# Later due times for the layer norms' powers in a planned attention and gated-graph kernel

## The chip, the cores and the metric

The kernel runs on one core of one Trainium2 chip. The metric is the device time of one execution in microseconds, as a median over runs. In the text PE is TensorE, DVE is VectorE, ACT is ScalarE, POOL is GpSimd and SP is SyncE. Of SyncE, only the issuing of DMAs matters here.

## The reference

The input x has shape (16, 1024, 128): 16 samples of 1024 nodes with 128 features. The matrix adj (1024 x 1024) holds zeros and ones. Two layers follow each other, each with a residual and a layer norm over the features:

```
h = x @ others_weight;  u1 = h @ a1;  u2 = h @ a2
e = leaky(u1[idx1] + u2[idx2]);  att = softmax(where(adj > 0, e, -9e15), axis=1)
x = layernorm(x + att @ h + x @ self_weight)            # layer 0

repeat 5 times, from h = x:                             # layer 1
    m = adj @ h             # both messages use the same adj
    z = sigmoid([m, m] @ w3.T + b3 + u);  r = sigmoid([m, m] @ w4.T + b4 + u);  u = h @ u3.T + bu3
    v = tanh([m, m] @ w5.T + b5 + (r * h) @ u5.T + bu5)
    h = (1 - z) * h + z * v
out = layernorm(x + h)
layernorm(x) = (x - mean(x)) / sqrt(var(x) + 1e-5)
```

Everything is float32.

## The kernel before

**Tiles and stages.** The 16 samples are called b. `layer0(b)` does the attention of one sample and its layer norm, which the profile calls "y". Layer 1 goes by pairs q of samples (2q, 2q + 1) and steps s from 0 to 4. `messages(q, s, k)` forms the products with adj for a pair; for most steps it saves multiplications by working with sums of blocks. `gates(b, s, soon)` does the gates r and z and the new state hT for each half e of the nodes. `leave(b, s)` brings the new state back into the other layout for the next step, through DRAM: VectorE transposes blocks of 32 (tile T), SyncE stores them (tile X), and the next step loads them as G. After the last step, `leave` adds the residual, which had been put aside in DRAM as yd, to give the tile o, and calls the layer norm "o". GpSimd then issues the output DMA. The last two samples take another way out (`end`).

**A layer norm** handles half a sample, 4 blocks of 128 nodes, in three operations on three engines. `look` (lines 527 and 529, VectorE) finds the mean and the variance. `power` (lines 533 to 543, GpSimd) makes rstd = (var + eps) to the power -0.5 and the bias. `scale` (line 548, ScalarE) applies them with four activations of 128 x 128. After a "y" scaling come the store of yd by GpSimd (L1009), the store of X by SyncE (L1023), and a block transpose on VectorE (tile T_b), which goes through DRAM (D_b, stored on L589, and F_b, loaded on L597) and becomes hT by a copy on ScalarE (L1037). After an "o" scaling comes only the output DMA (L1344). The tile o has two buffers. SyncE loads yd into it (L1324), and a pair needs four such halves.

**Order of the work.** No engine's order is written out by hand. Each operation is handed to `plan.add` with an engine, an assumed length in ns, a rank, and what it reads and writes. `Plan.order` simulates the engines with those lengths. When an engine is free, it takes the ready operation of the lowest rank for which buffers are free. The order of these starts is the program's order on every engine, and on the chip each engine keeps to it, waiting for semaphores. How long after an operation's assumed end its users count as ready is `LAG[engine]` (200 ns for POOL), unless the operation was given a `lag` of its own:

```
lag = self.SAME[engine] if ops[u][0] == engine else self.LAG[engine]
lag = self.lag.get(i, lag)
```

A `power` has an assumed length of 3001 ns (2301 in the short form, which only the last half of the last sample uses). Operations of VectorE and ScalarE get 10% on top of their assumed length, and TensorE's users of them 400 ns more (`CARE`).

**Names in the profile.** L621 is the helper `product` (all products with adj, and its sums), L1189, L1199, L1215 and L1216 are the gates' matmuls, L571 a transpose on TensorE. L1192 is the copy gz, L1114, L1141 and L1143 the copies of messages m, L1202 and L1221 the activations of the gates, L609 and L613 the two halves of a split for the products, L1083 a sum of G tiles. L1209, L1224, L1227 and L1230 are VectorE's part of the gates, with two inputs in SBUF each. L579 is the block transpose on VectorE.

Of the kernel before, what the change touches and what calls it, by code (L numbers as in the profile page):

```python
# [137 lines left out]
def kernel(  # L138
# [79 lines left out]
    def exact(pools):  # L218
# [67 lines left out]
        plan = Plan({tag: k[0] for tag, k in kinds.items()})  # L286
# [16 lines left out]
        D = dict(m=-0.8, pu=1.4, u=0.8, pr=0.8, pz=1.2, r=1.7, pv=1.0, z=1.3, hv=-0.4, h=1.2, tr=1.6, o=6.6, ln=2.9)  # L303
# [13 lines left out]
        def rank0(b):  # L317
            return 10 * (b // 2) - 1 * (1 - b % 2) + -1.0 - 6 * (b // 2 == 1)

        def sign(b):  # L320

            return 1 if b % 2 else -1
# [17 lines left out]
        def early_loads():  # L340
# [28 lines left out]
            writes=[(boot, "early"), (ws, "early"), (x0, "early"), (("xt", 1), "early"), *((t, "early") for k in staged for t in k)],  # L369
# [149 lines left out]
                dve(V, 1 + c / 4, sum_, reads=[*y, *more], writes=[(("tab",), c, n)])  # L519


        def layernorm(key, g, rank, after, src, dst, write, sg=1, short=False, later=()):
            stats, mv, rstd = ("stats", *key, g), ("mv", *key, g), ("rstd", *key, g)

            def look():
                for j in range(4):
                    nc.vector.bn_stats(T(stats)[:, j, :], src(j))
                for j in range(4):
                    nc.vector.bn_aggr(T(mv)[:, j, :], T(stats)[:, j, :])  # L529

            def power():
                mean, var, r = T(mv)[:, :, 0], T(mv)[:, :, 1], T(rstd)
                nc.gpsimd.tensor_scalar(r[:, 0, :], var, EPS, None, ALU.add)  # L533
                nc.gpsimd.tensor_tensor(r[:, 0, :], r[:, 0, :], mhalf[:, 0:4], ALU.pow)
                if short:
                    if sg < 0:
                        nc.gpsimd.tensor_scalar(r[:, 0, :], r[:, 0, :], -1.0, None, ALU.mult)
                elif sg > 0:
                    nc.gpsimd.tensor_scalar(r[:, 1, :], mean, -1.0, None, ALU.mult)
                    nc.gpsimd.tensor_tensor(r[:, 1, :], r[:, 1, :], r[:, 0, :], ALU.mult)  # L540
                else:
                    nc.gpsimd.tensor_tensor(r[:, 1, :], mean, r[:, 0, :], ALU.mult)
                    nc.gpsimd.tensor_scalar(r[:, 0, :], r[:, 0, :], -1.0, None, ALU.mult)

            def scale():
                r = T(rstd)
                for j in range(4):
                    nc.scalar.activation(
                        dst(j), src(j), AF.Identity, bias=r[:, 1, j : j + 1], scale=r[:, 0, j : j + 1]
                    )  # L550

            def scale_short():
                for j in range(4):
                    nc.vector.tensor_scalar(
                        dst(j), src(j), T(mv)[:, j, 0:1], T(rstd)[:, 0, j : j + 1], ALU.subtract, ALU.mult
                    )

            after = after if isinstance(after, list) else [after]
            dve(1100, rank, look, reads=after, writes=[(stats, 0), (mv, 0)])
            plan.add("POOL", 2301 if short else 3001, rank, power, reads=[(mv, 0)], writes=[(rstd, 0)])  # L560
            if short:
                dve(900, rank, scale_short, reads=[*after, (mv, 0), (rstd, 0)], writes=[write])
            else:
                act(1250, rank, scale, reads=[*after, *later, (mv, 0), (rstd, 0)], writes=[write])
# [66 lines left out]
        def layer0(b):  # L631

            first = rank0(b) - (60 if b == 0 else 0)
            rank = first + D["l1"]
# [9 lines left out]
            yT, y0, yd = ([(k, b, g) for g in range(2)] for k in ("yT", "y0", "yd"))  # L644
# [46 lines left out]
            if b >= 2:  # L691
# [6 lines left out]
                    reads=[(u, 0), (u, 1), (("ident",), 0)],  # L698
                    writes=[(put, 0)],
# [8 lines left out]
                    reads=[(us, 0)],  # L708
                    writes=[(ud, 0)],
# [5 lines left out]
                    reads=[(ud, 0)],  # L715
                    writes=[(pb, 0), (pb, 1)],
                    lag=3000,
# [66 lines left out]
            rank = first + D["l2"]  # L784
# [21 lines left out]
            rank = rank0(b) + D["l2"]  # L806
# [20 lines left out]
            for k in range(2 if b == 0 else 1):  # L827
                cs = slice(4 * k, 4 * k + 4) if b == 0 else slice(0, NC)

                def rz_(k=k, cs=cs):  # L830
# [16 lines left out]
                    reads=[(q, 0), *((zs, c) for c in ks), *((("A",), c, 1) for c in ks)],  # L847
                    writes=[(rz, k), (("bad",), k), (("rstd", "least"), k)] if b == 0 else [(rz, 0), (rz, 1)],
# [3 lines left out]
            rank = rank0(b) + D["l3"]  # L852
# [28 lines left out]
            rank = rank0(b) + D["l4"]  # L881
# [81 lines left out]
            for g in range(2):  # L963
                rank = rank0(b) + D["l5"]

                def y(g=g):
                    return T(yT[g])

                t = ("ps", "t", b, "y", g)
                if on_pe(b, "y"):  # L970
                    transposes(y, [(yT[g], 0)], t, rank)
                else:
                    k, d, t = (x + (b, "y", g) for x in (("T",), ("D",), ("F",)))
                    turn(k, y, [(yT[g], 0)], rank)
                    away(k, d, rank)
                    back(d, t, rank)

                def src(j, t=t, flat=on_pe(b, "y")):
                    return T(t)[:, j * P : (j + 1) * P] if flat else chunks(T(t))[:, j]

                def dst(j, g=g, flat=on_pe(b, "y")):
                    c = T(y0[g])[:, j, :]
                    return c if flat else c.rearrange("p (a j) -> p a j", a=4)

                layernorm(("y", b), g, rank0(b) + D["l6"], (t, 0), src, dst, (y0[g], 0), sign(b))

            if not plain(b // 2, 0):

# [293 lines left out]
        def leave(b, s):  # L1282

            rank = rank_of(b, s)
            hT = ("hT", b)
            for g in range(2):

                def h(g=g):
                    return T(hT)[:, g * HALF : (g + 1) * HALF]

                k, d = ("T", b, s, g), ("X", b, s + 1, g)
                if s < STEPS - 1 and on_pe(b, s):
                    t = ("ps", "t", b, s, g)
                    transposes(h, [(hT, g)], t, rank + D["tr"])
                    split(
                        ("blk", b, "h", s + 1, g),
                        lambda t=t: T(t).rearrange("p (c a j) -> p c a j", c=4, a=4),
                        [(t, 0)],
                        rank_of(b, s + 1),
                    )  # L1300
                    continue
                if s < STEPS - 1:
                    turn(k, h, [(hT, g)], rank + D["tr"])
                    away(k, d, rank + D["tr"])
                    continue

                if b >= B - 2:
                    end(b, s, g, h, rank)
                    continue

                t = ("ps", "t", b, s, g)
                if on_pe(b, s):
                    transposes(h, [(hT, g)], t, rank + D["tr"])
                else:
                    t = ("F", b, s, g)
                    turn(k, h, [(hT, g)], rank + D["tr"])
                    away(k, d, rank + D["tr"])
                    back(d, t, rank + D["o"])

                o, yd = ("o", b, g), ("yd", b, g)  # L1320
                sp(
                    450,
                    rank + D["o"],
                    lambda o=o, yd=yd: nc.sync.dma_start(T(o).rearrange("p c d -> p (c d)"), T(yd)),  # L1324
                    reads=[(yd, 0), (hT, g)],
                    writes=[(o, "y")],
                )

                def last(t=t, o=o, flat=on_pe(b, s)):
                    x = T(o).rearrange("p c (a j) -> p c a j", a=4)  # L1330
                    n = T(t).rearrange("p (c a j) -> p c a j", c=4, a=4) if flat else chunks(T(t))
                    nc.vector.tensor_tensor(x, n, x, ALU.add)

                dve(V, rank + D["o"], last, reads=[(t, 0), (o, "y")], writes=[(o, "raw")])

                def at(j, o=o):
                    return T(o)[:, j, :]

                layernorm(("o", b), g, rank + D["ln"], (o, "raw"), at, at, (o, 0), sign(b))
                plan.add(  # L1340
                    "POOL",
                    900,
                    rank + D["out"],
                    lambda o=o, g=g: nc.gpsimd.dma_start(  # L1344
                        out[b].rearrange("(c p) d -> p c d", p=P)[:, 4 * g : 4 * g + 4, :], T(o)
                    ),
                    reads=[(o, 0)],
                    writes=[((o, "sent"), 0)],
                    lag=2600,
                )  # L1350
# [347 lines left out]
```

## Time and profile before

| what | value |
|---|---|
| median of 3 runs | 1460.33 us (1458.93 to 1460.43) |
| the profiled execution | 1468.01 us, span 1466.2 us |
| TensorE busy | 1440.4 us, 98% of the span |
| VectorE busy | 1160.1 us, 79% |
| ScalarE busy | 896.2 us, 61% |
| GpSimd busy | 203.3 us, 14% |
| granted TensorE clock, mean | 0.994 |
| DMA | 174.20 MB, 119 GB/s |

The span is the time from the first to the last instruction of the profiled execution, which took somewhat longer than the runs without the profiler. A busy share is a mean over all stages. TensorE's busy time contains the modelled ends of its matmuls, so its short gaps are better read from the starts of the matmuls. A line of waits names the waiting engine, its tile and line, who ended the wait, and then the total in us, how often, and the longest.

### The profile page before, as it was taken

The numbers are of one execution on the slowest core, as the hardware profiler recorded it, in microseconds if no ns is written. First come the engines' busy times: TensorE is split into PE (matmuls) and PEld (weight loads), VectorE is DVE, ScalarE is ACT, GpSimd is POOL, SyncE is SP. The second block draws the span as 40 slices with busy tenths as digits, with TensorE's granted clock in tenths as the row PEclk, the third lists the DMA queues.
The fourth block names the chain that finished last, engine by engine and source line by source line (L and its number), as shares of the span: only waits on it lengthen the run. The fifth ranks groups of instructions, "written<-read, shape, count | busy, mean of one in ns | idle before, by whom it ended". The sixth has DMA issues, their size and how long they took to land.

```text
span 1466.2 us, 17789 instructions
## 1 busy us (share of the span) xinstructions
PE 1440.4 (98%) x5020; PEld 902.3 (62%) x5020; DVE 1160.1 (79%) x2753; ACT 896.2 (61%) x1792; POOL 203.3 (14%) x323
## 2 busy tenths in 40 slices
PE   9999999998999999999999999999999999999996
PEld 7766656665566656666666656656566656556663
DVE  5997789868888789987888788896988877776535
ACT  5656465665657665666657576566655656664544
POOL 0311001012101150110201112011200123000201
PEclk9999999999999999999999999999999999999998
DMA  7426135554434643455434543445432554223201
GB/s 250 145 55 205 52 102 150 137 158 116 112 100 137 184 126 90 121 163 150 108 108 123 158 129 101 115 143 159 123 89 79 150 166 129 58 72 87 72 0 31
DMA packets 188032, 174.20 MB, mean 119 GB/s; under 512 B 34239, under 2 KB 137366, under 8 KB 187926
## 3 DMA queue, kind: packets, MB, share of 16 engines
q1 hardware_dynamic: 182562, 156.41, 37.8%
q0 software_dynamic: 4800, 15.73, 3.2%
q8 instruction: 41, 0.67, 0.2%
q10 hardware_dynamic: 564, 0.85, 0.2%
q14 instruction: 65, 0.53, 0.1%
HBM read 95.68 MB, written 77.24 MB: 118 GB/s over the span
## 4 chain that ended last, share of the span: by engine, by line
PE 88%; DVE 4%; DMA 2%; SPq 1%; ACT 1%; issue 1%; POOL 1%; DVEq 0%; POOLq 0%; ACTq 0%
PE ps_acc_a L621 16%; PE ps_g_r L1199 8%; PE ps_g_v L1215 8%; PE ps_g_v L1216 8%; PE gz L1199 8%; PE ps_g_r L1189 8%; PE ps_acc_c L621 8%; PE ps_acc_po L621 8%; PE ps_acc L621 5%; PE gz L621 4%; PE ps_g_ph L658 1%; PE ps_idle L419 1%; SPq L589 1%; PE ps_acc_px L925 1%; PE ps_acc_po L939 1%
## 5 line engine op out<-in xcount | busy, mean ns | idle before, releaser
L1215 PE MATMUL ps_g_v<-m,wm 128*128 128x512 f32 x320 | 163.5, 592 | 0.1
L1216 PE MATMUL ps_g_v<-r,u5h 128*128 128x512 f32 x320 | 163.4, 592 | 0.0
L1199 PE MATMUL ps_g_r<-m,wm 128*128 128x512 f32 x320 | 160.0, 593 | 2.6 <-ACT gz L1192 2.6
L1199 PE MATMUL gz<-m,wm 128*128 128x512 f32 x320 | 159.5, 592 | 0.0
L1189 PE MATMUL ps_g_r<-hT,u 128*128 128x512 f32 x320 | 153.3, 592 | 0.0
L1224 DVE TENSOR_TENSOR hv<-hv,hT 128x512 f32<-128x512 f32 x160 | 109.8, 686 | 51.5 <-ACT hv L1221 51.0
L621 PE MATMUL ps_acc_a<-tab,blk_s 128*128 128x512 f32 x544 | 148.6, 415 | 1.6 <-ACT m L1141 1.6
L1209 DVE SCALAR_TENSOR_TENSOR r<-r,hT 128x512 f32<-128x512 f32 x160 | 109.2, 685 | 51.3 <-ACT r L1202 51.0
L1202 ACT ACTIVATE r<-ps_g_r,bh 128x512 f32<-128x512 f32 x160 | 109.1, 687 | 66.4 <-PE ps_g_r L1199 66.1
L621 PE MATMUL ps_acc_po<-adj,blk 128*128 128x512 f32 x512 | 141.5, 423 | 0.0
L1202 ACT ACTIVATE z<-gz,bh 128x512 f32<-128x512 f32 x160 | 109.6, 687 | 24.5 <-PE gz L1199 24.0
L621 PEld LDWEIGHTS ps_acc_a<-tab,blk_s 128*128 128x128 f32 x544 | 101.1, 188 | 37.5 <-issue 11.1
L621 PEld LDWEIGHTS ps_acc_po<-adj,blk 128*128 128x128 f32 x512 | 95.9, 188 | 36.6 <-issue 12.5
L1230 DVE SCALAR_TENSOR_TENSOR hT<-hv,hT 128x512 f32<-128x512 f32 x160 | 108.7, 681 | 2.2
L1227 DVE SCALAR_TENSOR_TENSOR hv<-z,hv 128x512 f32<-128x512 f32 x160 | 108.4, 678 | 2.1 <-ACT z L1202 1.1
L1192 ACT COPY gz<-ps_g_r 128x512 f32<-128x512 f32 x160 | 91.0, 572 | 29.7 <-PE ps_g_r L1189 28.2
L533 POOL TENSOR_SCALAR rstd_y<-mv_y 128x4 f32<-128x4 f32 x32 | 13.5, 422 | 682.1 <-DVE mv_y L529 657.6
L1216 PEld LDWEIGHTS ps_g_v<-r,u5h 128*128 128x128 f32 x320 | 60.6, 189 | 76.8 <-issue 61.1
L1199 PEld LDWEIGHTS gz<-m,wm 128*128 128x128 f32 x320 | 60.5, 190 | 76.4 <-issue 76.4
L621 PE MATMUL ps_acc<-adj,blk_h 128*128 128x512 f32 x384 | 101.3, 414 | 0.0
L609 ACT CAST blk_s<-G 128x512 fp32r<-128x512 f32 x136 | 82.3, 617 | 30.8 <-DVE G L1083 29.2
L613 DVE TENSOR_TENSOR blk_s<-G,blk_s 128x512 fp32r<-128x512 f32 x136 | 92.0, 681 | 8.7 <-ACT blk_s L609 8.2
(191 smaller groups left out, 2595.4 us busy)
## 6 DMA issues: line engine op xcount, KB each, us to landing
G<-X SPq DMA_DIRECT2D x140, 256.0 KB, 2.9
X<-T SPq DMA_DIRECT2D x552, 64.0 KB, 1.8
yd<-y POOLq DMA_DIRECT2D x32, 256.0 KB, 3.3
D_y<-T_y SPq DMA_DIRECT2D x112, 64.0 KB, 1.8
F_y<-D_y SPq DMA_DIRECT2D x28, 256.0 KB, 2.7
X<-y SPq DMA_DIRECT2D x28, 256.0 KB, 2.0
D_b<-T_b SPq DMA_DIRECT2D x112, 64.0 KB, 2.2
F_b<-D_b SPq DMA_DIRECT2D x28, 256.0 KB, 3.0
```

Source lines behind the costliest of these rows:

```text
L613: lambda: nc.vector.tensor_tensor(half(1), src(), half(0), ALU.subtract),
L621: nc.tensor.matmul(T(bank), T(blk)[:, k, c, :], right(c), start=(first and i == 0), stop=(last and i == len(terms) - 1), skip_group_check= ...
L1189: nc.tensor.matmul(T(pr), u3, h(), start=True, stop=True)
L1192: nc.scalar.copy(T(pz), T(pr))
L1199: nc.tensor.matmul(T(p_), wm[:, j, :], T(m), start=False, stop=True, skip_group_check=True)
L1202: nc.scalar.activation(T(t), T(p_), AF.Tanh, bias=bh[:, j : j + 1], scale=0.5 * sg)
L1209: lambda r=r, h=h: nc.vector.scalar_tensor_tensor(T(r), T(r), 1.0, h(), ALU.add, ALU.mult),
L1215: nc.tensor.matmul(T(pv), wm[:, 2, :], T(m), start=True, stop=False)
L1216: nc.tensor.matmul(T(pv), u5h, T(r), start=False, stop=True)
L1224: nc.vector.tensor_tensor(T(hv), T(hv), h(), ALU.subtract)
L1227: nc.vector.scalar_tensor_tensor(T(hv), T(z), 1.0, T(hv), ALU.add, ALU.mult)
L1230: nc.vector.scalar_tensor_tensor(h(), T(hv), 0.5, h(), ALU.mult, ALU.add)
```

## The change

The function `layernorm` gets an argument `calm`, which goes to the planner as the lag of the `power` operation, in place of the 200 ns of `LAG["POOL"]`. The "y" norms of the samples from 4 on get 1201 ns, those before keep 200 ns. The "o" norms that `leave` issues get 4001 ns. Those of the last two samples (in `end`) keep 200 ns. With the length of 3001 ns, the planner lets a scaling start 4.2 us and 7.0 us after its power's start, where it was 3.2 us. No instruction, tile, buffer or rank in the text of the program is touched; the planner draws the order of all engines anew from these times.

```diff
-        def layernorm(key, g, rank, after, src, dst, write, sg=1, short=False, later=()):
+        def layernorm(key, g, rank, after, src, dst, write, sg=1, short=False, later=(), calm=None):
...
-            plan.add("POOL", 2301 if short else 3001, rank, power, reads=[(mv, 0)], writes=[(rstd, 0)])
+            plan.add(
+                "POOL", 2301 if short else 3001, rank, power, reads=[(mv, 0)], writes=[(rstd, 0)], lag=calm
+            )
...
-                layernorm(("y", b), g, rank0(b) + D["l6"], (t, 0), src, dst, (y0[g], 0), sign(b))
+                layernorm(("y", b), g, rank0(b) + D["l6"], (t, 0), src, dst, (y0[g], 0), sign(b), calm=1201 if b >= 4 else None)
...
-                layernorm(("o", b), g, rank + D["ln"], (o, "raw"), at, at, (o, 0), sign(b))
+                layernorm(("o", b), g, rank + D["ln"], (o, "raw"), at, at, (o, 0), sign(b), calm=4001)
```

## The prediction

> **What bounds the kernel now.** I read the page first, then TensorE's waits, then ScalarE's waits, then the chain of work around each place where TensorE stands.
>
> ```profile
> span 1466.2 us, 17789 instructions
> PE 1440.4 (98%) x5020; PEld 902.3 (62%) x5020; DVE 1160.1 (79%) x2753; ACT 896.2 (61%) x1792; POOL 203.3 (14%) x323
> ```
>
> TensorE is busy for 98% of the span; no other engine is over 79%. An edit that adds and removes no TensorE work can only move the 26 us (1466.2 - 1440.4) in which TensorE stands. The view by stretches says where those are: 3.1 us in the first 40 us, 13.6 us in the last 26.2 us (1440 to 1466.2), and only some 9 us in the 1400 us between. Who ends TensorE's waits:
>
> ```profile
> PE ps_acc_a L621 <- ACT m L1143: 4.4, 1, 4.4
> PE ps_t L571 <- DVE hT L1230: 3.0, 3, 1.5
> PE ps_g_r L1199 <- ACT gz L1192: 2.6, 2, 1.7
> PE ps_acc_a L621 <- ACT m L1141: 1.6, 2, 1.1
> ```
>
> (Columns: total us, times, longest us.) Apart from the transposes at the very end (L571), TensorE waits for a copy by ScalarE, so I ask what ScalarE was doing. Its waits that this change touches:
>
> ```profile
> ACT o L548 <- POOL rstd_o L543: 10.7, 6, 5.5
> ACT o L548 <- POOL rstd_o L540: 9.8, 7, 4.5
> ```
>
> Thirteen times ScalarE stands in front of a layer norm's scaling (L548) until GpSimd has made rstd. The costliest case in the chain of work:
>
> ```profile
> 332.30 4.79 POOL rstd_o L533
> 337.17 1.05 POOL rstd_o L534
> ...
> 339.25 1.25 ACT o L548 x3
> 340.50 0.57 ACT hv L1221
> 341.07 0.49 ACT m L1143
> ...
> 341.60 3.59 PE ps_acc_a L621 x8
> ```
>
> (Start us, us, what.) GpSimd's power, then the scaling, then the copy m queued behind it, then TensorE, which had stood 4.37 us. The first GpSimd instruction took 4.79 us here, against 0.22 or 0.56 us in most others. VectorE's timeline shows why it ended when it did:
>
> ```profile
> 336.31 0.69 DVE L1227 SCALAR_TENSOR_TENSOR hv<-z,hv 128x512 f32<-128x512 f32 x1
> 336.91 0.71 DVE L579 STREAM_TRANSPOSE T<-hT 128x512 f32<-128x512 f32 x1
> ```
>
> From 332.12 us VectorE ran operations with two SBUF inputs without a break; the transpose at 336.91 is the first with one input, and GpSimd's instruction ended at 337.08. It is the same at 521.63 (4.18 us; the transpose starts at 525.65) and at 538.74 (2.99 us; transpose at 541.57).
>
> **What the Trainium skill says.** "SBUF — State Buffer", section "Who interferes with whom": a VectorE instruction with two SBUF inputs contends with a GpSimd instruction that reads SBUF. The three cases agree. So the power's time is set by VectorE's order and can't be one number: over the 32 norms "o" I read 1.95 to 6.58 us for the full chains, median 2.7, three above 3.3 (5.68, 6.51, 6.58). "TensorE: Matmul & The Clock Gate", section "What's actually happening": the array falls to half its clock after an idle window of about 3.4 us. The trace agrees: after the 4.37 us of idleness the granted clock was 0.53 from 342.0 to 345.5 us, and the eight matmuls at 341.60 took 3.59 us instead of 1.87.
>
> **The change part by part.** No instruction is added or removed; no tile, pool or DMA either. Two numbers move in the planner, which writes each engine's order.
>
> 1. *The "o" norms (28, those of b below 14).* The planner reckons rstd ready 3001 + 200 ns after the power starts; from now on 3001 + 4001 = 7.0 us. Measured worst: 6.58. A scaling then stands behind up to 3.8 us more of ScalarE's work (at 0.57 to 0.69 us per copy or activation, five or six of them), so that work no longer queues behind a wait. I summed TensorE's lost time from its matmul starts, against the usual spacing (0.234 us for the products of L621, 0.429 us for the gates). At 336.6: 4.54 us of gap, plus 1.65 us over the next nine matmuls at half clock. At 529.0: 1.88 plus 0.10 us. At 546.3: 0.68 plus 0.10 us. Sum 8.95 us, and in all three the chain runs through the power. The other ten waits (20.5 less 5.46, 3.45 and 4.49 = 7.1 us of ScalarE) cost TensorE nothing; other matmuls cover them. Gain: -8.95 us, between -8.95 and 0.
>
> 2. *The "y" norms of b = 4 to 15 (24).* From 3.2 to 4.2 us. Their waits since 245 us are 1.4 us in two, with no TensorE time lost, so there is nothing to gain; they measure at most 3.32 us. Behind each scaling follow GpSimd's store yd, SyncE's store X (L1023), VectorE's T_b turn and its four DMAs D_b, then F_b and the copy hT. Mostly this chain is covered by the products of the pair before. At the last entry it isn't: the scaling at 1192.25, T_b at 1193.98, D_b at 1196.50, F_b at 1201.48 with 3.26 us to land, hT at 1204.76, copy m, and TensorE stood 1.26 us until 1205.91. There 1.0 us later is 1.0 us lost. Cost: +1.0 us, between 0 and +1.0.
>
> 3. *All orders after the first moved scaling.* The planner is a list scheduler: one due time moves, and every later choice on PE, DVE, ACT, POOL and SP may fall differently. The first moved scaling is that of b = 4 or the first "o", so up to about 245 us (the first "y" power with the new time can't come before) the order should be nearly the old one. What a redrawn order costs no row shows; I bound it by stalls of other causes in this trace. From 245 to 1440 us they are 1.4 us. From 40 to 245 us they are 2.0 us (116 us: 0.84; 139 us: 1.12), a rate that gives 12 us over 1195 us. I take 4 us, nearer the longer stretch: +2.6 us net, between -1.4 and +10.6.
>
> SyncE's issues move with it. Each output DMA follows its scaling, so "o" tiles (two buffers for a pair's four halves) come free up to 3.8 us later; the load of the third and fourth half (L1324) waits for them at the head of SyncE's queue, with loads of G and stores of X behind it. The planner also counts the buffer as held longer and puts the load later, so I book nothing; the cover is the G loads' lead over their products. Uncovered, it is the slower rival below.
>
> Sum: -8.95 + 1.0 + 2.6 = -5.35 us. The profiled execution took 1468.01 us (span 1466.2 and 1.8 around it), so its span would be 1460.9. The unprofiled median is 1460.33, 7.7 lower; these stalls don't depend on the profiler as far as this shows, so I take the same difference: **1455.0 us**.
>
> **Rivals.** *Stalls that move.* ScalarE's waits go, but the redrawn order makes about as many elsewhere: -8.95 + 1.0 + 7 to 8, 1460 us. For it: VectorE at 79% can hold GpSimd anywhere, and 1.4 us of other stalls in 1195 us is little for an order that knows nothing of that. Against it: the planner leaves 400 ns of care between ScalarE or VectorE and TensorE. If the scalings don't move at all, because nothing else was ready for ScalarE, the time is also 1460; but right behind each of the three bad waits stood ready copies.
>
> *SyncE blocked by the output (slower).* In before, L1324 waits for the output DMA 48.8 us in 13 waits, longest 8.2. Fourteen such loads by 3.8 us make 53 us more of a blocked SyncE. If 8.95 of these 53 us (one in six) reach TensorE as late G or X, the gain is gone; at one in four, 13 us, the time is 1460.33 - 8.95 + 13 + 1 = 1465, more if gaps exceed 4 us and the clock falls. For it: SyncE is in order, and ScalarE waited 26.8 us in 23 times for G by DMA already. Against it: TensorE waited for none of those.
>
> **How the numbers follow.** A difference under 0.2% (2.9 us) can't be told from none here. Stalls gone, few new: 0.55, with 1451 to 1457 as its own range. Stalls moved or order unchanged: 0.16. SyncE blocked, or a redrawn order with over 12 us of new stalls: 0.29. These are the chances of faster, same and slower. The low end, 1450, is the whole gain with the 1.4 us of other stalls gone too and no cost of the y norms (1460.33 - 8.95 - 1.4); the high end, 1470, is the slower rival with about 5 us above its point. Outside lie some 0.05 below and 0.12 above.
>
> **What would show it.** Right: ScalarE's waits for rstd_o fall from 20.5 us to under 5, the longest to under 2; slow first instructions of over 2.5 us may still occur on GpSimd but no TensorE gap of over 2 us follows them; granted clock stays near 1.00 from 245 to 1440 us; TensorE busy stays at about 1440 us. Step 2: the last hT copy waits up to 1 us longer for F_b. Wrong: new TensorE waits on copies m or gz behind a wait for G by DMA (the slower rival, with L1324's waits above 48.8 us), or behind another scaling (the stalls moved).

## The result, and the profile after

The changed kernel takes 1456.13 us (median of 20 runs, 1454.19 to 1463.01), the kernel before 1460.38 us (20 runs, 1456.05 to 1464.61). The ratio is 0.9975, with a 95% interval of 0.9966 to 0.9983: faster by 4.2 us by the medians, a quarter of a per cent (2.5 to 5.0 us by the interval). The forecast was 1455.0.

The profiled execution took 1455.01 us. From its page, the span, the busy times and the engines' shares of the chain that ended last (88% PE before):

```profile
span 1452.9 us, 17795 instructions
PE 1434.8 (99%) x5020; PEld 899.5 (62%) x5020; DVE 1161.8 (80%) x2753; ACT 897.2 (62%) x1792; POOL 195.0 (13%) x323
...
PE 96%; DVE 1%; DMA 1%; ACT 1%; issue 0%; SPq 0%; POOL 0%; POOLq 0%; DVEq 0%; ACTq 0%
```

(Each engine's count is that of before; the six instructions more than the 17789 before are none of those counted as busy.)

TensorE's waits, all that the view of waits has (total us, times, longest):

```profile
PE ps_t L573 <- DVE hT L1232: 2.9, 2, 1.5
PE gz_fill L423 <- POOL ones L389: 1.4, 1, 1.4
PE ps_p L737 <- DVE T_ws L404: 1.1, 1, 1.1
PE ps_g_r L1201 <- ACT gz L1194: 0.7, 1, 0.7
PE ps_ahead L455 <- DVE blk L870: 0.6, 1, 0.6
PE ps_g_ph L660 <- ACT hx L670: 0.4, 1, 0.4
```

(The lines are two higher than before.) Each of these lies in the first 140 us or in the last 17 us. The wait for a copy m, 4.4 us before, is gone. Among ScalarE's waits only one for an rstd of an "o" norm is left, and it is the last sample's, which the change doesn't touch:

```profile
ACT y_o L548 <- POOL rstd_o L540: 5.1, 1, 5.1
```

This profile and the first one differ by 13.3 us of span, the medians by 4.2. The first profile of the kernel before came from an execution (1468.01 us) longer than any of the others. The 13.3 us are therefore not the gain, and two more profiles of the kernel before were taken; they stand further down.

To compare profiles I leave out the first 140 us, in which the loads at the start move everything by up to 3.5 us from execution to execution. Near 139 us TensorE waits for the same copy gz in every trace. "Rest" below is the time from the gate matmul that follows (ps_g_r) to the end of the span. It is the time of one execution, so it need not agree with the ratio of the medians beside it. A gap of TensorE is, here and below, the time between the starts of two matmuls beyond their usual spacing; it comes out some 0.16 us longer than the wait in the view of waits.

| kernel | ratio to before, 95% interval | rest in its profile, us |
|---|---|---|
| before, first profile | | 1326.0 |
| before, second and third | | 1318.5, 1318.8 |
| changed (two profiles) | 0.9975, 0.9966 to 0.9983; again 0.997, 0.9962 to 0.9977 | 1315.2, 1314.8 |
| only "o" later | 0.9996, 0.9986 to 1.0005 | 1321.5 |
| only "y" later | 1.0007, 0.9995 to 1.0018 | 1322.0 |
| old order, no wait for rstd | 0.9994, 0.9982 to 1.0006 | 1318.2 |
| old order, scalings moved by hand | 1.0048, 1.003 to 1.0066 | 1328.1 |
| changed, 1401 ns for "y" | 0.9982, 0.997 to 0.9994 | 1315.8 |
| power twice, before | 1.0123, 1.0108 to 1.0138 | 1333.1 |
| power twice, changed | 0.9977, 0.9969 to 0.9985 | 1315.4 |
| before, 221 ns for "o" | 0.999, 0.9976 to 1.0003 | 1316.1 |
| changed, 5001 ns for "o" | 1.0003, 0.9991 to 1.0014 | 1320.4 |

The order moved by hand has 6 runs, "power twice, before" only 4, of which the profiled one is the fastest (1473.40 us).

Some 1315 us is the rest without gaps: the changed kernel has none over 0.3 us between 140 and 1430 us. In the other profiles the rest is what their gaps make it. I take off their gaps over 0.2 us, and 1.7 us for each stretch of 3.4 us in which TensorE was granted half its clock. Such a stretch stands once in the first profile of before, in "only o", in "only y" and in the order moved by hand, and twice in "power twice, before". What is left is 1314.8 to 1315.9 us everywhere but in the order moved by hand (1316.9).

### The profile page after: what moved, and what is told of

It reads as the page before. It is cut to its first block, busy times and chain, and to the rows that moved or that the text cites. A ratio compares the mean times of both kernels' runs of the same rounds, so it can differ in the third digit from the quotient of the medians.

```text
span 1452.9 us, 17795 instructions
## 1 busy us (share of the span) xinstructions
PE 1434.8 (99%) x5020; PEld 899.5 (62%) x5020; DVE 1161.8 (80%) x2753; ACT 897.2 (62%) x1792; POOL 195.0 (13%) x323
## 4 chain that ended last, share of the span: by engine, by line
PE 96%; DVE 1%; DMA 1%; ACT 1%; issue 0%; SPq 0%; POOL 0%; POOLq 0%; DVEq 0%; ACTq 0%
PE ps_acc_a L623 17%; PE ps_g_r L1191 9%; PE ps_g_r L1201 9%; PE gz L1201 9%; PE ps_g_v L1217 9%; PE ps_g_v L1218 9%; PE ps_acc_c L623 9%; PE ps_acc_po L623 8%; PE ps_acc L623 6%; PE gz L623 4%; PE ps_g_ph L660 2%; PE ps_acc_px L927 1%; PE ps_acc_po L941 1%; PE ps_idle L419 1%; PE ps_t L573 1%; PE ps_ahead L455 0%
## 5 line engine op out<-in xcount | busy, mean ns | idle before, releaser
L623 PE MATMUL ps_acc_po<-adj,blk 128*128 128x512 f32 x512 | 137.7, 417 | 0.0
```

Of the source, the lines that this page charges most:

```text
L623: nc.tensor.matmul(T(bank), T(blk)[:, k, c, :], right(c), start=(first and i == 0), stop=(last and i == len(terms) - 1), skip_group_check= ...
```

## The experiments

**The theories.** "Cover" means that a scaling stands so late in ScalarE's order that its power is done when its turn comes. A "redraw" is a new order of all engines from the planner, a "draw" one such order. A: the power is covered, and the 8.95 us of the first profile are the gain. B: the redrawn order is what counts, and could have fallen otherwise. C, D and E came later and stand in the expectations.

**Each half of the change.** The "o" norms alone:

```diff
-                layernorm(("y", b), g, rank0(b) + D["l6"], (t, 0), src, dst, (y0[g], 0), sign(b), calm=1201 if b >= 4 else None)
+                layernorm(("y", b), g, rank0(b) + D["l6"], (t, 0), src, dst, (y0[g], 0), sign(b), calm=None)
```

> The 'o' norms keep their 4001 ns; the 'y' norms go back to 200 ns. Theory A (a scaling that stands behind the power's real time no longer holds ScalarE): all of the gain lies here, 2.5 to 5.5 us below the kernel before, and ScalarE's waits for rstd_o fall from 20.5 us to under 6 (5.1 of it at the very end). Theory B (the redrawn order is a lucky one): this is another redraw, so the time can fall anywhere within 5 us above or below before, whatever the waits do.

Measured 1460.22 us against 1460.91: no gain. All "o" waits for rstd are gone, as A said, but the time isn't. TensorE has new gaps; the largest is 1.75 us at 709 us, with another of 0.49 us right behind. In this kernel's timeline ScalarE waits at that point for a G load:

```profile
710.28 0.62 ACT L611 CAST blk_x<-G 128x512 fp32r<-128x512 f32 x1 [4.85 <-DMA G<-X]
```

And SyncE's waits from 692 to 712 us, with its timeline (start us, us issuing):

```profile
SPq L1326 <- DMA out_dram<-o: 10.0, 1, 10.0
```

```profile
702.55 0.33 SPq L1326 DMA_DIRECT2D o<-yd  x1
702.93 4.30 SPq L591 DMA_DIRECT2D X<-T  x8
707.57 1.47 SPq L599 DMA_DIRECT2D G<-X  x2
```

SyncE stood 10.0 us in front of the load of an "o" tile, because the output DMA of the tile's last user had not landed. The eight stores of X and the loads of G that followed came late, and TensorE behind them. That is the slower rival of the prediction, seen in one place. TensorE then ran at half its clock for 3.4 us, which costs another 1.7 us (stretch, its length, busy us of PE, PEld, DVE, ACT and POOL, granted clock, share and GB/s of DMA):

```profile
712.90:716.30 3.40, 3.40 (x9) 2.64 (x9) 3.40 (x7) 1.25 (x3) 0.00 (x0) 0.51 0.44 78
```

The prediction looked for the half clock behind some 3.4 us of idleness; here it came behind less. It did not come behind every such gap: after one of 1.98 us at 336 us in the order moved by hand, and one of 2.23 us at 335 us in "power twice, before", the granted clock stayed at 1.00.

The "y" norms alone (`calm=4001` taken out at the "o" norms):

> Only the 'y' norms of b from 4 on get 1201 ns. Theory A: no gain, within 2 us of before, as ScalarE's waits for rstd_o stay near 20 us (10 to 30) and TensorE gaps behind them stay. Theory B: a full redraw from about 245 us on, so a gain of 4 us is as likely here as with the 'o' norms.

1462.15 against 1460.91 us, not to be told from no change. Its one large gap, 3.61 us at 879.6, has the same form: the "o" load at 876.64 had held SyncE for 5.7 us, G was issued at 877.15, and ScalarE waited 3.48 us for it before it came to the scaling and the copy gz:

```profile
876.64 0.34 SPq L1326 DMA_DIRECT2D o<-yd  x1
877.15 0.34 SPq L599 DMA_DIRECT2D G<-X  x1
```

```profile
880.18 0.62 ACT L611 CAST blk_x<-G 128x512 fp32r<-128x512 f32 x1 [3.48 <-DMA G<-X]
```

No "o" norm has a later due time here, and SyncE's waits for the output DMA are shorter in sum than before (41.4 against 48.8 us, the longest 8.2 in both). So this gap comes of the redraw, not of later outputs. So neither half carries the gain. Their sum doesn't either; the gain belongs to the order that both together draw.

**The old order without the wait.** The scalings read constants instead of rstd:

```diff
-                r = T(rstd)
+                r = mhalf.rearrange("p (t j) -> p t j", t=2) if key[0] == "o" and key[1] < 14 else T(rstd)
```

> The order of before on all engines. The scalings of the 'o' norms below b = 14 read constants in place of rstd, so that they wait for nothing on GpSimd; this part of the computation (the division by the standard deviation) is left out. Theory A: the gain of the change without any redraw, 3 to 6 us below before, up to 9 in a profile like that of before; the three TensorE gaps of 4.5, 1.9 and 0.7 us are gone, others stay. Theory B: no gain, within 2 us of before.

1459.58 against 1460.91 us, and by ratio 0.9 us less with an interval from 2.6 less to 0.9 more. Theory A falls: by the medians the waits for rstd cost about 1 us, not 8.95. In this run's own profile two powers were slow again (4.18 us for the first instruction at 513.2 us, 2.99 at 528.3), and with nobody waiting for them TensorE has no gap there. The control of the changed kernel on the same chip:

> The changed kernel as it is, beside the others on one chip. Both theories: 3 to 6 us below before. Theory A: equal to the one with only the 'o' norms within 2 us.

1456.52 us, the gain again in full.

**More profiles of the kernel before.**

> The kernel before, unchanged, for a second profile. Theory C (the three waits for rstd in the first profile were larger than in most executions): the waits of ScalarE for rstd_o sum to 8 to 15 us instead of 20.5, TensorE loses 1 to 4 us behind them instead of 8.95, and the span is 1456 to 1462 us. Theory A (8.95 us is what these waits cost in every execution): the same three TensorE gaps of 4.5, 1.9 and 0.7 us, span near 1464.

> The kernel before, unchanged, for a third profile; as for the second. Theory C: TensorE gaps behind rstd differ from profile to profile and stay under 4 us in sum. Theory A: the three gaps come back alike.

Theory C holds. ScalarE's waits of the second profile (1460.57 us, span 1458.8):

```profile
ACT o L548 <- POOL rstd_o L540: 8.6, 7, 3.9
...
ACT o L548 <- POOL rstd_o L543: 3.2, 5, 2.0
```

TensorE's waits in it, those for copies between 139 and 1430 us:

```profile
PE ps_g_r L1199 <- ACT gz L1192: 1.5, 2, 0.9
PE ps_acc_a L621 <- ACT m L1141: 1.0, 1, 1.0
PE ps_acc_a L621 <- ACT m L1143: 0.7, 2, 0.4
```

(Of the first line, 0.9 us is the wait near 139 us; the other stands at 321 us.)

Behind rstd TensorE lost 0.49 us (at 337 us), and 0.82 us in the third. The two other gaps of the first profile, at 529 and 546 us, aren't there at all, though ScalarE waited 3.9 us at the latter place: TensorE had other matmuls to run. More is lost at the last entry, near 1197 and 1202 us: 1.11 and 0.56 us in the second, 1.08 and 0.64 in the third. That is the F_b chain that my second step priced. The first of the two also stands in the first profile (1.26 us) and in the old order with constants for rstd (1.46 us). No redrawn order has either. How ScalarE meets the last two hT copies in the second profile of before:

```profile
1196.97 0.62 ACT L1037 COPY hT<-F_b 128x512 f32<-128x512 f32 x1 [3.76 <-DMA F_b<-D_b]
1202.06 0.62 ACT L1037 COPY hT<-F_b 128x512 f32<-128x512 f32 x1 [1.83 <-DMA F_b<-D_b]
```

And in the changed kernel:

```profile
1176.49 0.62 ACT L1039 COPY hT<-F_b 128x512 f32<-128x512 f32 x1 [0.18 <-DMA F_b<-D_b]
1177.83 0.62 ACT L1039 COPY hT<-F_b 128x512 f32<-128x512 f32 x1 [0.20 <-DMA F_b<-D_b]
```

The last scaling "y" starts at 1168.37 us there and at 1184.63 us in the second profile of before. The new order does the last sample's layer 0 earlier, so that F_b has landed when its copy's turn comes.

**The scalings alone, moved by hand.** The planner's order of before was kept on PE, DVE and SP; each "o" scaling, and where needed its output DMA with it, was put behind up to five of the next operations of ScalarE (it stops before an operation that takes a new tile o):

```diff
-            for i in plan.order():
+            for i in moved(plan.order()):
```

> The planner's order of before, with only the scalings of the 'o' norms below b = 14 moved behind the next five operations of ScalarE (their output DMAs with them); PE, VectorE and SyncE keep their order. Theory A: 3 to 6 us below before. Theory B and C: the cover alone is worth 1 to 2 us below before, as with constants in place of rstd; ScalarE's waits for rstd_o under 3 us apart from 5.1 at the end.

1468.5 against 1461.2 us: slower by 7 us, although ScalarE waits only 1.1 us for these rstd. All theories were wrong here. TensorE has three gaps of about 2 us: 1.98 at 336 us, 2.09 at 374 us and 2.30 at 1371 us. At 374 us, the VectorE, SyncE and TensorE timelines of this kernel show why:

```profile
373.43 0.69 DVE L1336 TENSOR_TENSOR o<-F,o 128x512 f32<-128x512 f32 x1 [4.24 <-DMA o<-yd]
```

```profile
370.55 0.34 SPq L1328 DMA_DIRECT2D o<-yd  x1
```

```profile
376.41 1.90 PE L625 MATMUL ps_acc_c<-adj,blk_s 128*128 128x512 f32 x7 [1.93 <-DVE m L1155]
```

The same load and the same sum in the second profile of before:

```profile
366.46 0.37 SPq L1324 DMA_DIRECT2D o<-yd  x1
```

```profile
371.01 0.69 DVE L1332 TENSOR_TENSOR o<-F,o 128x512 f32<-128x512 f32 x1 [1.79 <-DMA o<-yd]
```

The scaling came later, so the output DMA landed later, so the tile came free later (SyncE's waits for out_dram are 66.8 us here, 44.3 in the second profile of before). The load of the next "o" half went out late, VectorE stood 4.24 us in front of the residual's sum, where it had stood 1.79, and the combination m behind it held TensorE. At 1371 us it is the same chain, by way of the new state hT: VectorE stood 3.05 and 2.08 us for two "o" loads, in the second profile of before 1.72 and 1.11. The gap at 336 us has another cause. ScalarE waited 3.24 us for VectorE before an activation hv; the scaling, which stood in that pause in the order of before, now follows the activation and stands for 1.64 us in front of the copy m that TensorE needs. The sum of SyncE's waits alone decides nothing, for the changed kernel has 63.1 us of them and no gap; what counts is what stands behind them. The planner, when it is told of the later power, moves these loads and sums as well. Without a redraw, this cover costs more than it saves.

**Other draws.** A later "y", a later "o", and a redraw without cover (`calm=221` for "o", none for "y"):

> The changed kernel with 1401 ns in place of 1201 for the 'y' norms: the scalings are covered as well, and the order is redrawn from 245 us on. Theory B (the clean order of the change is luck): new TensorE gaps of 2 to 6 us between 245 and 1430 us, time 1457 to 1462. Theory D (later 'y' and 'o' together keep ScalarE free in any order): no such gaps, within 1.5 us of the changed kernel.

> The changed kernel with 5001 ns in place of 4001 for the 'o' norms, 'y' as changed. Theory D (later 'y' and 'o' together keep the order free of gaps): within 1.5 us of the changed kernel. Theory B: gaps of 2 to 7 us between 245 and 1430 us, 1457 to 1463, though no scaling waits for rstd.

> The 'o' norms get 221 ns in place of 200: no cover to speak of, but another order of all engines. Theory B (a redraw alone moves the time by several us either way): TensorE gaps between 245 and 1430 us change place and sum to anything from 0 to 10 us, ScalarE still waits 10 us or more for rstd_o; 1456 to 1466. If only the cover counts: within 1 us of before.

1457.22 against 1461.2 us; 1460.95 and 1458.39 against 1460.61. The first can't be told from the change (by the ratio 2.6 us faster than before, 0.9 to 4.4), the second is no better than before: its gaps (0.89, 1.30, 0.58 and 1.40 us) come without any "o" scaling waiting for rstd, so theory D falls. Two of them have the cause seen above. At 709 us, before the gap of 1.30 us, SyncE stood in front of an "o" load and ScalarE then for G (SyncE's waits from 690 to 713 us, ScalarE's timeline):

```profile
SPq L1326 <- DMA out_dram<-o: 10.8, 1, 10.8
```

```profile
709.58 0.62 ACT L611 CAST blk_x<-G 128x512 fp32r<-128x512 f32 x1 [3.04 <-DMA G<-X]
```

At 1370 us, before the gap of 1.40 us, VectorE stood 2.46 us for an "o" load. The third, with 221 ns, still has its waits for rstd:

```profile
ACT o L548 <- POOL rstd_o L540: 6.6, 4, 4.1
...
ACT o L548 <- POOL rstd_o L543: 3.8, 4, 2.1
```

Yet it lost only 0.9 us at TensorE after 140 us (0.32, 0.28 and 0.26), and its median lies 1.5 us below before by the ratio, with an interval that just reaches no change. It has no gap at the last entry. So 21 ns in one due time did about as much as taking all these waits away in the old order; neither is clear of no change.

**Is the cover worth anything?** The power was lengthened in both kernels, in the same orders:

```diff
-                nc.gpsimd.tensor_scalar(r[:, 0, :], var, EPS, None, ALU.add)
-                nc.gpsimd.tensor_tensor(r[:, 0, :], r[:, 0, :], mhalf[:, 0:4], ALU.pow)
+                for again in range(2 if key[0] == "o" and key[1] < 14 else 1):
+                    nc.gpsimd.tensor_scalar(r[:, 0, :], var, EPS, None, ALU.add)
+                    nc.gpsimd.tensor_tensor(r[:, 0, :], r[:, 0, :], mhalf[:, 0:4], ALU.pow)
```

> The planner's order of before; on GpSimd each 'o' norm below b = 14 does its first addition and its power twice, about 1.7 us more per norm (the output differs, since eps is added and the power taken twice). Theory E (the cover counts once the power is late): ScalarE's waits for rstd_o grow from some 13 us to 30 to 50, TensorE loses 4 to 15 us more, 1464 to 1475. If these waits are always hidden: within 1.5 us of before.

> The same doubling in the changed kernel, whose scalings stand up to 6.7 us after their power's end. Theory E: ScalarE's waits for rstd_o under 5 us besides 5.1 at the end, and within 2 us of the changed kernel, 1455 to 1459. Theory B (only the order's luck): it suffers like before, 4 us or more.

(The first expectation is mistaken in a detail: the second round starts from the variance again, so the output stays what it was.) Before goes to 1478.14 us, 17.5 more (four runs, 1473.4 to 1478.8; all of them lie above every run of before). The changed kernel takes 1457.67 us, 1.2 to 1.5 more than its medians with one power. ScalarE's waits in the lengthened kernel before:

```profile
ACT o L549 <- POOL rstd_o L541: 30.7, 12, 5.9
ACT o L549 <- POOL rstd_o L544: 18.2, 12, 3.9
```

In the lengthened changed kernel no such line is left but that of the last sample:

```profile
ACT y_o L549 <- POOL rstd_o L541: 5.1, 1, 5.1
```

So the cover is real, and of great worth where the power is late. With the power as it is, it costs TensorE much only in some executions, such as the first profile.

## Why the prediction was right in its number and wrong in three of its terms

The number (1455.0, measured 1456.13), the direction, and the narrower range (1451 to 1457) held. The sum behind them was not right: large errors of opposite sign offset each other. That the number came out so near was luck. The forecast change, -5.35 us, lies just outside the measured interval of -2.5 to -5.0.

*Step 1, the "o" norms: mis-sized.* I took 8.95 us as what the waits for rstd cost in every execution. In the second and third profiles they cost TensorE 0.49 and 0.82 us, and taking them away in the old order is worth 0.9 us (2.6 less to 0.9 more). The mechanism as described stands: the doubled power shows it. What failed was reading its size from one profile whose own time, 7.7 us above the median, I had put down to the profiler, as I had under the table of the profile before. It was the sign that this execution had more stalls: the later profiles run at the time of the other runs (1460.57 and 1460.49 us), and their rests are 7.5 and 7.2 us shorter.

*Step 2, the "y" norms: wrong sign.* I priced the F_b chain at the last entry at +1.0 us. It is the right place: the old order loses about 1.7 us there. The redraw took it away: the scaling there came about 16 us earlier on the clock of the profile (1168.37 against 1184.63), not 1 us later.

*Step 3, the redraw: wrong sign here.* I booked +2.6 us within -1.4 to +10.6. The changed order has no such gaps, so those of the last entry (1.7 us), near 1367 us (0.26 and 0.47) and at 320 us (0.72 and 0.21) go as well: -2.65 us by the second profile and -2.4 by the third, which includes step 2's place and lies below my bound. With step 1 at 0.5 to 0.8 us the gaps make 3.1 to 3.2 us of the 3.5 to 3.8 by which the rests differ (against the mean of the two changed profiles); the medians differ by 4.2 us. The other draws, in which the planner chose, lie by their medians from 4 us faster to 1 us slower than before; 12 us of new stalls came in none. I could not have worked out from the profile where this one would fall.

*SyncE's issues: booked at nothing.* In the changed kernel that holds: its waits for the output DMA grew from 48.8 to 63.1 us, the longest from 8.2 to 12.3, and no TensorE gap follows. It fails in the kernels with only "o" or only "y" later, with 5001 ns for "o", and in the order moved by hand: a SyncE held by an "o" load made the largest gap of each. The slower rival named the right mechanism, though not for this draw.

*The signs.* The waits for rstd of the 28 "o" norms are gone, and up to 245 us the "y" norms follow each other at the old distances. No slow first GpSimd instruction came in this execution (0.71 us at most), so its cover wasn't tested until the power was doubled; in "only o" one took 3.58 us at 686 us, and no scaling waited. TensorE's busy time fell to 1434.8 us, where I expected 1440. The later profiles of before have 1435.9 and 1437.7, so the 1440.4 belonged to the first execution; its stretch at half clock, counted as busy, is 1.7 us of it.

*Open.* Why the first execution of before met three slow powers and the next two only one is not shown. Nor is it shown what makes one draw free of gaps and its neighbour not; the runs show the gaps' causes, not a rule for avoiding them.

## What to carry to other kernels

When a planner writes the order, move an operation through its due time and let everything be planned anew: such a move made by hand on one engine cost 7 us, in two of its three large gaps because loads and buffers did not follow. A later due time buys cover against a late power (doubled, it costs 17.5 us in the old order and about 1.3 in the new), but no gain of its own: with "only o" all waits were gone and the time was not. Before pricing stalls, compare the profiled execution's own time with the median, and if it lies beyond the range of the others, take a second profile. Hold a change in such an order against some neighbours with other due times: here they lie between 4 us faster and 1 us slower with the same instructions.

## What the runs showed of the hardware that was not expected

How long VectorE's two-input operations hold a GpSimd instruction varies between executions of one program. The prediction said that the power's time is set by VectorE's order; the order was the same in these executions, and the time was not. The first instruction of one power, in the first and second profile of before and in the old order with constants for rstd:

```profile
521.63 4.18 POOL L533 TENSOR_SCALAR rstd_o<-mv_o 128x4 f32<-128x4 f32 x1 [1.85 <-DVE mv_o L529]
```

```profile
516.12 0.57 POOL L533 TENSOR_SCALAR rstd_o<-mv_o 128x4 f32<-128x4 f32 x1 [1.85 <-DVE mv_o L529]
```

```profile
513.19 4.18 POOL L533 TENSOR_SCALAR rstd_o<-mv_o 128x4 f32<-128x4 f32 x1 [2.56 <-DVE mv_o L529]
```

Each time the same unbroken row of two-input operations ran on VectorE, and it had begun 0.16 to 0.17 us earlier (at 521.46, 515.96 and 513.02 us). The slow ones ended when the next transpose had started; the quick one was let through within the row. Of these three and the third profile of before, the power at 332.3 us of the first profile was slow in one (4.78 us, 0.57 in the other three), this one in two, and the one at 538.7 us in all four (2.98 to 2.99 us). TensorE's cost behind rstd was 8.95 us in the first profile and 0.49 us in the second.
